# Sums of squares with the data as the stationary operand, and the engines that take the roots: a four-layer graph network on one core

## The chip, the cores and the metric

The kernel runs on one core of a Trainium2 chip. A core has five engines, each with its own in-order queue: TensorE (PE; its weight loads are shown as PEld), VectorE (DVE), ScalarE (ACT), GpSimd (POOL) and SyncE (SP), which here issues the transfers. The metric is the device time of one execution in microseconds, as a median over several runs.

## The reference, cut to what matters

64 graphs of 256 nodes with 128 features pass through four layers. Each layer's result is added to its input and normalised. What bears on this case:

```python
def _layernorm(x, axis=-1, eps=1e-5):
    return (x - mean(x)) / sqrt(var(x) + eps)

# layer 0: p = x (W1 - W2), q = x W2
h = max over j of relu(p_i + q_j + b) * adj[i, j]
# layer 1: three elu(x W + b), two products with adj, tanh of a product
# layer 2: a graph convolution with a normalised adjacency, used twice
A_hat = adj + eye;  deg = A_hat.sum(-1);  dinv = where(deg > 0, rsqrt(deg), 0)
norm_A = dinv[:, None] * A_hat * dinv[None, :]
# layer 3: one message per pair of nodes
pre = m_j[None, :, :] + m_i[:, None, :] + b1
msg = gelu(_layernorm(pre, g1, be1))          # variance over the 128 features
agg[i] = sum over j of msg[i, j] * adj[i, j]
x = _layernorm(x + _layernorm([x, agg] @ W2 + b2, g2, be2))
```

The adjacency holds zeros and ones, is symmetric, has a one on its diagonal, and about one entry in eight is set.

## The kernel before, in words

**Columns instead of pairs.** Layers 0 and 3 work on pairs of nodes. For each graph, and each half `h` (0 or 1) of its 256 source nodes, the target nodes are sorted by how many neighbours they have in that half (`perm`, `permT`). Then up to 40 slots are filled: slot `s` holds the `s`-th neighbour of each target, and as targets are sorted, high slots need few columns. All slots of one half stand side by side in 4800 columns (`WIDTH`), cut into tiles of 1024, 1024, 1024, 1024 and 704. `hot` is a matrix of zeros and ones, 128 sources by 4800 columns in fp8, made by DVE at L629 and L635; a product with `hot` gathers a neighbour's features into each column. A column whose target has fewer neighbours than its slot is empty: its column of `hot` is all zeros. `lack` (L591) says by how much a slot exceeds a target's count.

**Four stages.** `first` (L502) loads a graph, sorts, makes `hot` and does layer 0: three matmuls per 512 columns (L665), small ones that push empty columns far down (L681), and a running maximum on DVE (`fold`, L492). `second` is layer 1. `third` (L782) is layer 2 and the beginning of layer 3. `last` (L821) is the rest of layer 3 and the update. At any time the four stages work on four consecutive graphs. `together` (L341) takes the next piece of that stage which is least advanced by its share; the shares are the numbers of pieces in `STAGES` (L879), and a piece ends at a `yield`. This fixes, when the program is built, the order of the instructions on each engine. All graphs are unrolled.

**Layer 3 by tiles.** `TODO` lists ten tiles per graph (five per half). For each, `sums_of` (L718) gathers `c3` by three matmuls per 512 columns into a PSUM tile `bigp`, of which there are four (L728); DVE adds the target's part into `pre` (L732); ACT squares it into `sq` (L736). The features stand on the 128 partitions, so the sum over features is a product with ones: four matmuls per tile (L743), ones as the stationary operand (32 columns), a quarter of the squares as the moving one, each into its own 32 partitions of PSUM. ACT copies the sums into `row`, with 1/128 as scale and eps added (L745), and SP writes one row of each quarter to a line in DRAM (L750). After each second tile the line of both is read back across partitions, 16 values on each, as `vr` (L762); the mask `fu` comes beside it (L764); ACT takes the root and DVE the reciprocal (`inverse_root`, L72 to L75), DVE multiplies by the mask (L769), and the scales go to DRAM as `scale_line` (L771). `last` reads them back, broadcast to all partitions, as `rs_s` (`fetch`, L825), multiplies `pre` (L839), applies Gelu on ACT (L841) and sums over slots (`fold` again). `sums_of` runs four tiles ahead of this (`AHEAD`), and `fetch` two.

**The mask.** `first` compares `lack` with zero (L615) and writes the answer to DRAM in the order of the columns, in eight transfers (L620).

**Roots elsewhere.** `layernorm` (L166) adds eps on DVE (L174), yields, takes the root on ACT and the reciprocal on DVE, yields, and scales. It is called five times per graph. `layer_2` (L261) makes `dinv` from the degrees by the same `inverse_root`, adds the identity to `aT`, and scales `hs` by `dinv` on DVE before each of two products with `aT` (L293, L296). ACT keeps one set of functions loaded; where the next function is of another set, an ACT_TABLE_LOAD stands before it.

A second path, `general`, is there for inputs that the sparse one can't hold. It isn't run with these.

Of the kernel before, what the change touches and what calls it, by code (L numbers as in the profile page):

```python
# [19 lines left out]
P = 128  # L20
# [23 lines left out]
def kernel(  # L44
# [19 lines left out]
    make_identity(nc, ident)  # L64
    half = consts.tile([P, N], F32, name="half")
    nc.vector.memset(half, 0.5)
    eps_t = consts.tile([P, 1], F32, name="eps_t")
    nc.vector.memset(eps_t, EPS)
    minus1 = consts.tile([P, 1], F32, name="minus1")
    nc.vector.memset(minus1, -1.0)  # L70

    def inverse_root(t):  # L72

        nc.scalar.activation(t, t, AF.Sqrt)  # L74
        nc.vector.reciprocal(t, t)  # L75

# [80 lines left out]
    class Shared:  # L157
# [8 lines left out]
        def layernorm(self, dst, src, g=None, be=None):  # L166

            st = self.work.tile([P, H, 6], F32, name="st", bufs=4)
            mv = self.work.tile([P, H, 2], F32, name="mv", bufs=4)
            for h in range(H):  # L170
                nc.vector.bn_stats(st[:, h], src[:, h])
                nc.vector.bn_aggr(mv[:, h], st[:, h])
            rs = self.work.tile([P, H], F32, name="rs", bufs=4)
            nc.vector.tensor_scalar(rs, mv[:, :, 1], EPS, None, ALU.add)  # L174
            yield
            inverse_root(rs)
            yield
# [25 lines left out]
        def to_features(self, xn, name, bufs=None):  # L203

            pt = self.psum()
            for h in range(H):
                nc.tensor.transpose(pt[:, h * P:(h + 1) * P], xn[:, h], ident)
            t = self.state.tile([P, N], F32, name=name, **({"bufs": bufs} if bufs else {}))
            nc.scalar.copy(t, pt[:, :N])
            return t  # L210

        def node_tile(self, name):
# [47 lines left out]

        def layer_2(self, s, aT, deg_of):  # L261

            work, psum, elu = self.work, self.psum, self.elu
            x2 = s["x2"]
            deg = work.tile([P, H], F32, name="deg")
            deg_of(deg)
            nc.vector.tensor_scalar(deg, deg, 1.0, None, ALU.add)
            pos = work.tile([P, H], F32, name="pos")
            nc.vector.tensor_scalar(pos, deg, 0.0, None, ALU.is_gt)
            dinv = work.tile([P, H], F32, name="dinv")  # L270
            nc.vector.tensor_scalar(dinv, deg, 1e-30, None, ALU.max)
            inverse_root(dinv)
            yield
            nc.vector.tensor_mul(dinv, dinv, pos)
            for h in range(H):
                blk = aT[:, h, h * P:(h + 1) * P]
                nc.vector.tensor_add(blk, blk, ident)
            yield
            xT = self.to_features(x2, "xT_2", 1)
# [11 lines left out]
            for step in (1, 2):  # L291
                for h in range(H):
                    nc.vector.tensor_scalar(hs[:, h], hs[:, h], dinv[:, h:h + 1], None, ALU.mult)  # L293
                pa = psum()
# [59 lines left out]
    def sparse(ctx):  # L354
# [28 lines left out]
        def row_of(slot):  # L383
            return slot + 3 if slot < SLOTS - 1 else 0
# [109 lines left out]
        def split3(dst, src):  # L494
# [5 lines left out]
            nc.vector.tensor_sub(dst[:, 2], r, dst[:, 1])  # L500

        def first(g, s):  # L502

# [38 lines left out]
            nc.vector.scalar_tensor_tensor(kc, pc, -1.0, down_c, ALU.mult, ALU.subtract)  # L542
            dg = state.tile([P, H], F32, name="dg", bufs=3)
            nc.vector.tensor_reduce(dg, pc, AX.X, ALU.add)
            s["dg"] = dg

# [65 lines left out]
            s.update(an=an, aT=aT, perm=perm, permT=permT, lack=lack)  # L612

            full = pair.tile([ROWS, H, N], BF16, name="full")
            nc.vector.tensor_scalar(full, lack, 0.0, None, ALU.is_equal)  # L615
            s["fulls"] = fulls = dram.tile([H, WIDTH], BF16, name="fulls", bufs=5)
            for s0, n, w in RECTS:
                for a, m in ([(s0, n)] if s0 != g_s0 else [(s0, n - 1), (SLOTS - 1, 1)]):
                    at, r = SLOT_AT[a][0], row_of(a)
                    nc.sync.dma_start(  # L620
                        fulls[:, at:at + m * w].rearrange("h (s k) -> s h k", k=w), full[r:r + m, :, :w]
                    )
            yield
# [18 lines left out]
            yield  # L642
            s["hot"] = hot

            pq = psum()
# [66 lines left out]

        TODO = [(h, t0, tl) for h in range(H) for t0, tl in TILES]
        AHEAD = 4
        GROUP = 2
        PIECE = 16

        def sums_of(s, i):  # L718
# [5 lines left out]
            for b in range(0, tl, 512):  # L724
# [10 lines left out]
            sq = big.tile([P, TILE], F32, name="sq", bufs=1)  # L735
            nc.scalar.activation(sq[:, :tl], pre[:, :tl], AF.Square)  # L736
            yield

            bl = P if tl % 512 == 0 else tl // 4
            v4 = sq[:, :tl].rearrange("p (b q k) -> p b q k", q=4, k=bl)  # L740
            pr = psum()
            for q in range(4):
                nc.tensor.matmul(pr[q * Q:(q + 1) * Q, :tl // 4], ones[:, :Q], v4[:, :, q], start=True, stop=True)  # L743
            row = big.tile([P, TILE // 4], F32, name="row")
            nc.scalar.activation(row[:, :tl // 4], pr[:, :tl // 4], AF.Identity, bias=eps_t, scale=1.0 / P)  # L745
            at = sum(n for _, _, n in TODO[i - i % GROUP:i])
            if at == 0:
                s["line"] = dram.tile([1, GROUP * TILE], F32, name="line")
            line = s["line"]
            nc.sync.dma_start(  # L750
                line[:, at:at + tl].rearrange("o (b q k) -> (o q) b k", q=4, k=bl),
                row.rearrange("(q p) n -> q p n", p=Q)[:, 0, :tl // 4].rearrange("q (b k) -> q b k", k=bl),
            )
            yield
            if i % GROUP < GROUP - 1:
                return

            n = at + tl
            rows = n // PIECE
            first_at = TODO[i - GROUP + 1][0] * WIDTH + TODO[i - GROUP + 1][1]  # L760
            vr = big.tile([P, PIECE], F32, name="vr")
            nc.sync.dma_start(vr[:rows], line[:, :n].rearrange("o (p k) -> (o p) k", k=PIECE))  # L762
            fu = big.tile([P, PIECE], BF16, name="fu")
            nc.sync.dma_start(  # L764
                fu[:rows],
                s["fulls"].rearrange("h w -> (h w)")[first_at:first_at + n].rearrange("(p k) -> p k", k=PIECE),
            )
            inverse_root(vr[:rows])
            nc.vector.tensor_mul(vr[:rows], vr[:rows], fu[:rows])  # L769
            out_line = dram.tile([1, GROUP * TILE], F32, name="scale_line")  # L770
            nc.sync.dma_start(out_line[:, :n].rearrange("o (p k) -> (o p) k", k=PIECE), vr[:rows])  # L771
            at = 0
            for j in range(i - GROUP + 1, i + 1):
                s["scale", j] = out_line[:, at:at + TODO[j][2]]
                at += TODO[j][2]
            yield
# [5 lines left out]
        def third(g, s):  # L782

            dg = s["dg"]

            def deg_of(deg):
                nc.vector.tensor_scalar(deg, dg, 1.0 / N, None, ALU.mult)

            yield from sh.layer_2(s, s["aT"], deg_of)
            yield  # L790
# [30 lines left out]
        def last(g, s):  # L821
# [3 lines left out]
            def fetch(i):  # L825
                if i < len(TODO):
                    scale_of[i] = rs = big.tile([P, TILE], F32, name="rs_s", bufs=3)
                    nc.sync.dma_start(rs[:, :TODO[i][2]], s.pop(("scale", i)).broadcast_to([P, TODO[i][2]]))

# [48 lines left out]
        U = next(u for u in (UNROLL, 8, 4, 2, 1) if B % u == 0)  # L878
        STAGES = [(last, 34), (third, 34), (second, 14), (first, 44)]  # L879

# [14 lines left out]
    def general(ctx):  # L895
# [11 lines left out]
        psum = sh.psum  # L907
        ones3 = cs.tile([3, P], BF16, name="ones3")

        def split3(dst, src):  # L910
# [67 lines left out]
        def middle(g, s):  # L978
# [9 lines left out]

            def deg_of(deg):
                nc.vector.tensor_reduce(deg, an, AX.X, ALU.add)  # L990

            yield from sh.layer_1(s, an, aT, s["x1"])
            yield
            yield from sh.layer_2(s, aT, deg_of)
            yield

# [81 lines left out]
        def run():  # L1078
            nc.vector.memset(ones3, 1.0)

            with tc.For_i(0, B, U) as g0:
# [61 lines left out]
```

## Time and profile before

| what | value |
|---|---|
| median of three runs | 5727.86 us (5726.6 to 5728.21) |
| the profiled execution's own time | 5731.62 us |
| span from its first to its last instruction | 5729.7 us |
| mean granted clock of TensorE | 0.862 |
| DMA: mean busy share of the engines, rate | 20.0%, 63 GB/s |
| ACT_TABLE_LOAD at L841, L74, L194 | 535, 445, 221 of 1283 ns each |
| largest waits: ACT at L745 for L743 on PE | 476.7 us |
| PE at L296 for DVE at L293, at L769 | 214.8 us, 101.3 us |
| DVE at L839 for the transfer into rs_s | 48.0 us |

A line of groups gives the line of the code, the engine, the operation, output and input with their shapes, the count, then after the bar the busy time in us and the mean ns of one, then the idle time before them and what ended it. A line of the timeline gives the start in us, the length in us, the engine, the line, and how many instructions it merges. A line of stretches gives the stretch, its length, and the busy time of each engine in it, with counts in brackets, then the granted clock, the DMA share and the rate. Busy time of PE is the time in which at least one matmul is under way, from its start to its modelled end.

### The profile page before, as it was taken

To read this page: it belongs to the slowest core of one execution; us is meant where nothing else is said; L and a number is where in the kernel's file an instruction comes from. 1 tells how busy PE (TensorE), PEld (TensorE's weight loads), DVE (VectorE), ACT (ScalarE), POOL (GpSimd) and SP (SyncE) were. 2 spreads that over 40 slices of the span, in tenths; PEclk is the share of its full clock that TensorE was granted. 3 is DMA by queue.
4 is the path that set the end of the run, shared out by engine and by line. 5 is a ranking of instruction groups with operands and counts; after the bars stand their busy time and mean duration, and the time that the engine had idled before them with its cause. 6 is when DMAs were issued, how large, how long until landed. Compare 5 with 4: busy or idle time off the path is not lost.

```text
span 5729.7 us, 83531 instructions
## 1 busy us (share of the span) xinstructions
PE 4529.9 (79%) x27408; PEld 2508.7 (44%) x27408; DVE 4834.4 (84%) x14654; ACT 4275.2 (75%) x6485; POOL 1.9 (0%) x10
## 2 busy tenths in 40 slices
PE   5878878878778778788788788787887887877875
PEld 2444444444444444444444444444444444444443
DVE  6788888888888888888888888888888888888876
ACT  2577777777777777777777777777777777777785
POOL 0000000000000000000000000000000000000000
PEclk8888889889889889888898898898888887888986
DMA  0122222222212221221221222122212212221222
GB/s 22 44 70 63 62 63 72 62 63 66 69 57 70 65 63 63 72 63 62 63 72 62 63 65 70 59 68 65 63 62 72 64 62 63 69 66 60 68 65 74
DMA packets 292813, 365.15 MB, mean 64 GB/s; under 512 B 151952, under 2 KB 210448, under 8 KB 292368
## 3 DMA queue, kind: packets, MB, share of 16 engines
q1 hardware_dynamic: 292368, 359.73, 20.0%
q8 instruction: 217, 3.56, 0.3%
q14 instruction: 228, 1.87, 0.1%
HBM read 345.07 MB, written 14.53 MB: 63 GB/s over the span
## 4 chain that ended last, share of the span: by engine, by line
PE 52%; DVE 29%; ACT 11%; issue 4%; DMA 3%; SPq 0%; DVEq 0%; POOL 0%; ACTq 0%
PE bigp L665 11%; PE bigp L728 8%; DVE pre L839 6%; PE mm L860 5%; DVE lanes L492 4%; PE mm L743 4%; DVE hot L629 4%; DVE pre L732 4%; DVE sums L492 3%; PE bigp L681 3%; DMA rs_s<-scale_line 2%; PE mm L870 2%; PE mm L296 2%; PE mm L699 2%; PE mm L647 2%
## 5 line engine op out<-in xcount | busy, mean ns | idle before, releaser
L665 PE MATMUL bigp<-hot,q 128*128 128x512 fp8e4 (+1 forms) x3840 | 1052.3, 371 | 66.6 <-DVE lanes L492 52.6
L728 PE MATMUL bigp<-hot,c 128*128 128x512 fp8e4 (+1 forms) x3840 | 928.8, 372 | 140.2 <-DVE pre L732 140.2
L732 DVE TENSOR_TENSOR pre<-bigp,dT 128x512 f32<-128x512 f32 (+6 forms) x1664 | 846.3, 530 | 37.8 <-PE bigp L728 33.5
L492 DVE TENSOR_TENSOR lanes<-bigp,lanes 128x512 f32<-128x512 f32 (+6 forms) x1536 | 772.7, 503 | 94.6 <-PE bigp L681 86.9
L839 DVE TENSOR_TENSOR pre<-pre,rs_s 128x1024 f32<-128x1024 f32 (+1 forms) x640 | 732.9, 1150 | 48.6 <-DMA rs_s<-scale_line 48.0
L736 ACT ACTIVATE sq<-pre 128x1024 f32<-128x1024 f32 (+1 forms) x640 | 638.5, 998 | 169.9 <-DVE pre L732 163.9
L841 ACT ACT_TABLE_LOAD x535 | 686.4, 1283 | 9.5
L492 DVE TENSOR_TENSOR sums<-pre,sums 128x1024 f32<-128x1024 f32 (+6 forms) x1024 | 628.8, 614 | 41.2 <-ACT pre L841 40.7
L745 ACT ACTIVATE row<-mm,eps_t 128x256 f32<-128x256 f32 (+1 forms) x640 | 289.6, 453 | 476.9 <-PE mm L743 476.7
L841 ACT ACTIVATE pre<-pre,be,g 128x1024 f32<-128x1024 f32 (+1 forms) x512 | 594.2, 1172 | 57.8 <-DVE pre L839 53.0
L743 PE MATMUL mm<-sq,ones 128*32 128x256 f32 (+1 forms) x5120 | 482.9, 440 | 135.2 <-ACT sq L736 135.2
L74 ACT ACT_TABLE_LOAD x445 | 570.9, 1283 | 7.5
L728 PEld LDWEIGHTS <-c 128*128 128x128 bf16 x3840 | 331.2, 98 | 550.5 <-issue 136.1
L665 PEld LDWEIGHTS <-q 128*128 128x128 bf16 x3840 | 310.8, 97 | 392.6 <-issue 112.0
L296 PE MATMUL mm<-aT,hs 128*128 128x256 f32 x512 | 232.3, 600 | 316.1 <-DVE hs L293 214.8
L629 DVE TENSOR_SCALAR hot<-rank 128x512 fp8e4<-128x512 bf16 (+5 forms) x1536 | 440.5, 348 | 0.0
L681 PEld LDWEIGHTS <-pick 42*128 42x128 bf16 x2944 | 155.8, 95 | 481.5 <-issue 474.2
L296 PEld LDWEIGHTS mm<-aT,hs 128*128 128x128 f32 x512 | 135.6, 293 | 425.8 <-issue 316.1
L860 PE MATMUL mm<-w3u,sums 128*128 128x128 f32 x2048 | 296.7, 289 | 18.4 <-DVE sums L492 16.1
L194 ACT ACT_TABLE_LOAD x221 | 283.5, 1283 | 3.9
L681 PE MATMUL bigp<-lack,pick 42*128 42x36 bf16 (+16 forms) x2944 | 285.7, 187 | 0.0
L860 PEld LDWEIGHTS mm<-w3u,sums 128*128 128x128 f32 x2048 | 254.5, 195 | 37.3 <-issue 17.6
(226 smaller groups left out, 7132.6 us busy)
## 6 DMA issues: line engine op xcount, KB each, us to landing
rs_s<-scale_line SPq DMA_DIRECT2D x512, 512.0 KB
rs_s<-scale_line SPq DMA_DIRECT2D x128, 352.0 KB
an<-in_adj SPq DMA_DIRECT2D x64, 256.0 KB
x<-in_x SPq DMA_DIRECT2D x64, 128.0 KB
line<-row SPq DMA_DIRECT2D x512, 4.0 KB
out<-o SPq DMA_DIRECT2D x64, 128.0 KB
fu<-fulls SPq DMA_DIRECT2D x192, 4.0 KB
vr<-line SPq DMA_DIRECT2D x192, 8.0 KB
```

The lines of the kernel that those rows point to most:

```text
L74: nc.scalar.activation(t, t, AF.Sqrt)
L492: nc.vector.tensor_tensor(lanes[:, :k, :w], src[:, i:i + k], lanes[:, :k, :w], op)
L629: nc.vector.tensor_scalar(hot[:, :, at:at + w], rank[:, :, :w], s0 + i + 1.0 - FAR, None, ALU.is_equal, saturate=False)
L665: nc.tensor.matmul(pt[:, :tl], q3[:, i, h], hot[:, h, t0:t0 + tl], start=i == 0, stop=False)
L681: nc.tensor.matmul(o_, l_, r_, start=False, stop=i == len(todo) - 1)
L728: nc.tensor.matmul(pt[:, :bl], c3[:, k, h], hot[:, h, t0 + b:t0 + b + bl], start=k == 0, stop=k == 2)
L732: nc.vector.tensor_add(block(pre[:, b:], n, w, at), block(pt, n, w, at), widen(dT[:, h, :w], n))
L736: nc.scalar.activation(sq[:, :tl], pre[:, :tl], AF.Square)
L743: nc.tensor.matmul(pr[q * Q:(q + 1) * Q, :tl // 4], ones[:, :Q], v4[:, :, q], start=True, stop=True)
L839: nc.vector.tensor_mul(pre[:, :tl], pre[:, :tl], rs[:, :tl])
L841: nc.scalar.activation(msg[:, :tl], pre[:, :tl], AF.Gelu, bias=be3, scale=g3)
L860: nc.tensor.matmul(pt[:, cols], lanes[:, k, cols], w3u[:, 1], start=k == 0, stop=False)
```

## The change

1. The squares become the stationary operand. `sums_of` picks every eighth column of `sq` from column `b` on, for `b` from 0 to 7 (`PIECE`), as a stationary block of 128 columns, and multiplies by one column of ones. The sums come out with 128 columns of the tile on the partitions and eight per partition, in the arrangement that `vr` had after its way through DRAM. ACT copies them into `vr` (scale and eps as before). The lines `line`, `row` and `fu` and their transfers go.
2. The mask comes from `hot` itself: its column sums by TensorE, 80 matmuls per graph of the same kind with two columns of ones, copied by DVE into `filled`. The comparison and the eight transfers go, and `first` has one piece more (45).
3. The scales' root is one POOL instruction (power -0.5), and the product with the mask is POOL's too. Each tile has its own scale line.
4. `dinv` is made in `first`, with the power on POOL, and scales `aT` once instead of `hs` twice.
5. The norms' root stays on ACT, with eps as its bias; the add on DVE goes, and the reciprocal moves past a yield.
6. `sq` has two buffers instead of one.

```diff
     def inverse_root(t):
-        nc.scalar.activation(t, t, AF.Sqrt)
-        nc.vector.reciprocal(t, t)
+        nc.gpsimd.tensor_tensor(t, t, mhalf[:t.shape[0], :t.free_size()], ALU.pow)
...
+            yield
             rs = self.work.tile([P, H], F32, name="rs", bufs=4)
-            nc.vector.tensor_scalar(rs, mv[:, :, 1], EPS, None, ALU.add)
-            yield
-            inverse_root(rs)
-            yield
+            nc.scalar.activation(rs, mv[:, :, 1], AF.Sqrt, bias=eps_t)
+            yield
+            nc.vector.reciprocal(rs, rs)
...
+        def inverse_root_of(self, deg, bufs):
+            nc.vector.tensor_scalar(deg, deg, 1.0, None, ALU.add)
+            pos = self.work.tile([P, H], F32, name="pos")
+            nc.vector.tensor_scalar(pos, deg, 0.0, None, ALU.is_gt)
+            dinv = self.state.tile([P, H], F32, name="dinv", bufs=bufs)
+            nc.vector.tensor_scalar(dinv, deg, 1e-30, None, ALU.max)
+            inverse_root(dinv)
+            nc.gpsimd.tensor_mul(dinv, dinv, pos)
+            return dinv
...
+            for h in range(H):
+                nc.vector.tensor_scalar(aT[:, h], aT[:, h], dinv[:, h:h + 1], None, ALU.mult)
...
             for step in (1, 2):
-                for h in range(H):
-                    nc.vector.tensor_scalar(hs[:, h], hs[:, h], dinv[:, h:h + 1], None, ALU.mult)
...
-            full = pair.tile([ROWS, H, N], BF16, name="full")
-            nc.vector.tensor_scalar(full, lack, 0.0, None, ALU.is_equal)
-            s["fulls"] = fulls = dram.tile([H, WIDTH], BF16, name="fulls", bufs=5)
...
+            pf = psum()
+            for i, (h, t0, tl) in enumerate(TODO):
+                for b in range(PIECE):
+                    c = (i * PIECE + b) * 2
+                    nc.tensor.matmul(
+                        pf[:tl // PIECE, c:c + 2], hot[:, h, t0 + b:t0 + tl:PIECE], ones_b[:, :2], start=True, stop=True
+                    )
+            filled = hold.tile([P, H, len(TILES), PIECE], F32, name="filled")
...
+        def scale_root(t, full):
+            nc.gpsimd.tensor_tensor(t, t, mhalf3[:t.shape[0], :t.shape[1]], ALU.pow)
+            nc.gpsimd.tensor_mul(t, t, full)
...
             pr = psum()
-            for q in range(4):
-                nc.tensor.matmul(pr[q * Q:(q + 1) * Q, :tl // 4], ones[:, :Q], v4[:, :, q], start=True, stop=True)
-            row = big.tile([P, TILE // 4], F32, name="row")
-            nc.scalar.activation(row[:, :tl // 4], pr[:, :tl // 4], AF.Identity, bias=eps_t, scale=1.0 / P)
...
+            rows = tl // PIECE
+            for b in range(PIECE):
+                nc.tensor.matmul(pr[:rows, b:b + 1], sq[:, b:tl:PIECE], ones[:, :1], start=True, stop=True)
+            if i % GROUP == 0:
+                s["vr"] = big.tile([P, GROUP, PIECE], F32, name="vr")
+            vr = s["vr"]
+            nc.scalar.activation(vr[:rows, i % GROUP], pr[:rows, :PIECE], AF.Identity, bias=eps_t[:rows], scale=1.0 / P)
...
+            for j in range(i0, i + 1):
+                s["scale", j] = line = dram.tile([1, TILE], F32, name="scale_line")
+                nc.sync.dma_start(
+                    line[:, :TODO[j][2]].rearrange("o (p k) -> (o p) k", k=PIECE), vr[:all_rows[j - i0], j - i0]
+                )
...
-        STAGES = [(last, 34), (third, 34), (second, 14), (first, 44)]
+        STAGES = [(last, 34), (third, 34), (second, 14), (first, 45)]
```

More of the change, by code (lines that the diff above doesn't have):

```diff
@@ L64 @@
     make_identity(nc, ident)
-    half = consts.tile([P, N], F32, name="half")
-    nc.vector.memset(half, 0.5)
     eps_t = consts.tile([P, 1], F32, name="eps_t")
@@ L70 @@
     nc.vector.memset(minus1, -1.0)
+    mhalf = consts.tile([P, 16], F32, name="mhalf")
+    nc.vector.memset(mhalf, -0.5)
+    mhalf3 = mhalf.rearrange("p (a b) -> p a b", a=2)
     def inverse_root(t):
-        nc.scalar.activation(t, t, AF.Sqrt)
-        nc.vector.reciprocal(t, t)
+        nc.gpsimd.tensor_tensor(t, t, mhalf[:t.shape[0], :t.free_size()], ALU.pow)
     def load(src, shape, name):
@@ L259, in layer_1, with layer_2 @@
             s["x2"] = x2
-        def layer_2(self, s, aT, deg_of):
+        def layer_2(self, s, aT, dinv_of):
             work, psum, elu = self.work, self.psum, self.elu
             x2 = s["x2"]
[L265 to L272, printed above, removed]
+            dinv = dinv_of()
             yield
-            nc.vector.tensor_mul(dinv, dinv, pos)
             for h in range(H):
@@ L500, in split3 @@
             nc.vector.tensor_sub(dst[:, 2], r, dst[:, 1])
+        TODO = [(h, t0, tl) for h in range(H) for t0, tl in TILES]
+        AHEAD = 4
+        GROUP = 2
+        PIECE = 8
         def first(g, s):
@@ L542, in first @@
             nc.vector.scalar_tensor_tensor(kc, pc, -1.0, down_c, ALU.mult, ALU.subtract)
-            dg = state.tile([P, H], F32, name="dg", bufs=3)
+            dg = work.tile([P, H], F32, name="dg")
             nc.vector.tensor_reduce(dg, pc, AX.X, ALU.add)
-            s["dg"] = dg
+            nc.vector.tensor_scalar(dg, dg, 1.0 / N, None, ALU.mult)
+            s["dinv"] = sh.inverse_root_of(dg, 4)
             more = work.tile([P, H, H], F32, name="more")
@@ L612, in first @@
             s.update(an=an, aT=aT, perm=perm, permT=permT, lack=lack)
-            full = pair.tile([ROWS, H, N], BF16, name="full")
-            nc.vector.tensor_scalar(full, lack, 0.0, None, ALU.is_equal)
-            s["fulls"] = fulls = dram.tile([H, WIDTH], BF16, name="fulls", bufs=5)
[L617 to L622, printed above, removed]
             yield
@@ L643, in first @@
             s["hot"] = hot
+            pf = psum()
[6 more added lines that the diff above has]
+            filled = hold.tile([P, H, len(TILES), PIECE], F32, name="filled")
+            pfv = pf[:, :2 * len(TODO) * PIECE].rearrange("p (h t b two) -> p h t b two", h=H, b=PIECE, two=2)[..., 0]
+            rows = TILES[-1][1] // PIECE
+            last_t = len(TILES) - 1
+            nc.vector.tensor_copy(filled[:, :, :last_t], pfv[:, :, :last_t])
+            nc.vector.tensor_copy(filled[:rows, :, last_t], pfv[:rows, :, last_t])
+            s["filled"] = filled.rearrange("p h t b -> p (h t) b")
+            yield
             pq = psum()
@@ L711, in first @@
             yield from sh.layernorm(s["x1"], y)
[L713 to L716, printed above, removed]
+        def scale_root(t, full):
+            nc.gpsimd.tensor_tensor(t, t, mhalf3[:t.shape[0], :t.shape[1]], ALU.pow)
+            nc.gpsimd.tensor_mul(t, t, full)
         def sums_of(s, i):
@@ L734, in sums_of @@
                     )
-            sq = big.tile([P, TILE], F32, name="sq", bufs=1)
+            sq = big.tile([P, TILE], F32, name="sq")
             nc.scalar.activation(sq[:, :tl], pre[:, :tl], AF.Square)
             yield
-            bl = P if tl % 512 == 0 else tl // 4
-            v4 = sq[:, :tl].rearrange("p (b q k) -> p b q k", q=4, k=bl)
             pr = psum()
-            for q in range(4):
-                nc.tensor.matmul(pr[q * Q:(q + 1) * Q, :tl // 4], ones[:, :Q], v4[:, :, q], start=True, stop=True)
-            row = big.tile([P, TILE // 4], F32, name="row")
-            nc.scalar.activation(row[:, :tl // 4], pr[:, :tl // 4], AF.Identity, bias=eps_t, scale=1.0 / P)
[L746 to L753, printed above, removed]
+            rows = tl // PIECE
[5 more added lines that the diff above has]
+            nc.scalar.activation(vr[:rows, i % GROUP], pr[:rows, :PIECE], AF.Identity, bias=eps_t[:rows], scale=1.0 / P)
             yield
@@ L756, in sums_of @@
                 return
[L758 to L775, printed above, removed]
+            i0 = i - GROUP + 1
+            all_rows = [TODO[j][2] // PIECE for j in range(i0, i + 1)]
+            parts = [(all_rows[0], 0, GROUP)] if len(set(all_rows)) == 1 else [
+                (r, j, j + 1) for j, r in enumerate(all_rows)
+            ]
+            for r, lo, hi in parts:
+                scale_root(vr[:r, lo:hi], s["filled"][:r, i0 + lo:i0 + hi])
+            for j in range(i0, i + 1):
[3 more added lines that the diff above has]
+                )
             yield
@@ L782, in third @@
         def third(g, s):
[L784 to L789, printed above, removed]
+            yield from sh.layer_2(s, s["aT"], lambda: s["dinv"])
             yield
@@ L827, in fetch @@
                     scale_of[i] = rs = big.tile([P, TILE], F32, name="rs_s", bufs=3)
-                    nc.sync.dma_start(rs[:, :TODO[i][2]], s.pop(("scale", i)).broadcast_to([P, TODO[i][2]]))
+                    nc.sync.dma_start(rs[:, :TODO[i][2]], s.pop(("scale", i))[:, :TODO[i][2]].broadcast_to([P, TODO[i][2]]))
             for i in range(2):
@@ L908, in general @@
         ones3 = cs.tile([3, P], BF16, name="ones3")
+        half = cs.tile([P, N], F32, name="half")
         def split3(dst, src):
@@ L987, in middle, with dinv_of @@
             yield
-            def deg_of(deg):
+            def dinv_of():
+                deg = work.tile([P, H], F32, name="deg")
                 nc.vector.tensor_reduce(deg, an, AX.X, ALU.add)
+                return sh.inverse_root_of(deg, 1)
             yield from sh.layer_1(s, an, aT, s["x1"])
             yield
-            yield from sh.layer_2(s, aT, deg_of)
+            yield from sh.layer_2(s, aT, dinv_of)
             yield
@@ L1079, in run @@
             nc.vector.memset(ones3, 1.0)
+            nc.vector.memset(half, 0.5)
             with tc.For_i(0, B, U) as g0:
```

## The prediction

> **What bounds the kernel now.** I read the page's first two parts, then the busy time by stretch of one graph's interval, then single rows for prices. The program repeats per graph: the four matmuls of L566 start first at 43.2 us and last at 5456.2 us (view of that line), (5456.2 - 43.2) / 63 = 85.9 us per graph. I cut one interval, 2853.44 to 2939.44 us, where PE's character changes.
>
> ```profile
> PE 4529.9 (79%) x27408; PEld 2508.7 (44%) x27408; DVE 4834.4 (84%) x14654; ACT 4275.2 (75%) x6485; POOL 1.9 (0%) x10
> ```
> ```profile
> 2853.44:2857.44 4.00, 4.00 (x11) 3.28 (x11) 1.71 (x4) 0.63 (x3) 0.00 (x0) 0.50 0.50 166
> 2857.44:2905.44 48.00, 47.32 (x315) 26.60 (x318) 43.00 (x131) 34.13 (x49) 0.00 (x0) 1.00 0.23 69
> 2905.44:2939.44 34.00, 18.02 (x110) 9.06 (x109) 29.72 (x95) 31.66 (x51) 0.00 (x0) 0.80 0.13 42
> ```
> The columns are the length, then busy time of PE, PEld, DVE, ACT, POOL, then the granted clock. The average (PE 79%) hides two stages. In the 48 us, **stage A**, PE is covered for 47.3 and DVE for 43.0: these two set the pace and ACT (34.1) follows. In the 34 us, **stage B**, ACT (31.7) and DVE (29.7) set it and PE is half idle. PE's cover in A is flattered, because pipelined matmuls overlap. Counting its matmuls there by column count at their dense spacing (512 columns of fp8: 0.216 us, the median from start to start of L665; fp32 128 columns: 0.111) gives 38.5 us, of which the sums of squares (L743) are 2.2. So A has 9.5 us in which PE streams nothing.
>
> **The sums of squares on PE.** Before, one tile of 1024 columns costs eight matmuls that run four abreast:
>
> ```profile
> L743 PE MATMUL mm<-sq,ones 128*32 128x256 f32 (+1 forms) x5120 | 482.9, 440 | 135.2 <-ACT sq L736 135.2
> 2811.18 0.64 PE L743 MATMUL mm<-sq,ones 128*32 128x256 f32 x8
> ```
> That is 482.9 / 64 = 7.5 us per graph. After, the data are stationary: eight blocks per tile, each an fp32 block of 128 columns picked with a step of 8 elements, streaming one column. Every fp32 matmul here is two instructions (L743: 5120 for 640 x 4), so 16 load-and-multiply pairs per tile, 11 equivalents in the two 704-column tiles (88 of 128 stationary columns): 8 x 16 + 2 x 11 = 150 per graph. With one column to stream, a pair costs its weight load. The rows that price it:
>
> ```profile
> 2808.97 0.97 PEld L870 LDWEIGHTS mm<-ak,permT 128*128 128x128 f32 x8
> L870 PEld LDWEIGHTS mm<-ak,permT x1024: 186/192/333, 278.9 to 5718.2; 128*128 128x128 f32 x171
> 2835.44 1.16 PE L566 MATMUL mm<-perm,nz 128*128 128x256 bf16 x4 [4.15 <-DVE perm L560]
> L488 DVE TENSOR_REDUCE part_max<-bigp x128: 344/357/358, 64.8 to 5518.6; 128x12 f32<-128x192 f32 x128
> L488 DVE TENSOR_REDUCE part_add<-pre x128: 448/476/491, 253.9 to 5707.4; 128x12 f32<-128x192 f32 x128
> ```
> Contiguous fp32 loads follow each other every (0.97 - 0.192) / 7 = 0.111 us: the lower end. No row has a weight load with a 32-byte step. Two rows show what steps do to reads. L566 streams 256 bf16 columns 4 bytes apart: (1.16 - 0.372) / 3 = 0.263 us each, 1.03 ns per element; 128 elements make 0.131. L488 reduces 192 elements with a step of 48 bytes: 476 ns from SBUF; the same shape from PSUM takes 357. A two-element reduce takes 152 (L544), so SBUF costs (476 - 152) / 192 = 1.69 ns per element; 128 make 0.216: the upper end. I take **0.216**, because its step passes 16 bytes as the new one does (32), and L566's 4 do not. Per graph: 150 x 0.111 = 16.7, x 0.131 = 19.7, x 0.216 = 32.4 us, in place of 7.5.
>
> The Trainium skill (SBUF — State Buffer, Door 1: The DMA port swizzle) speaks against the change: SBUF has 16-byte lines, fp32 strides of up to four elements are free, and each access to a new line pays. It names no size. By it the load is above 0.111 us; L488 agrees in direction, and no run here shows it for TensorE.
>
> **Stage A, the term that decides.** Six of a graph's ten tiles lie there (48 weight loads of L743), 96 pairs. PE's dense sum without the old ones is 38.5 - 2.2 = 36.3. With them: 47.0 at 0.111, 48.9 at 0.131, 57.0 at 0.216. At 0.216 PE alone passes the stage's 48 us. A burst is 16 x 0.216 = 3.5 us, while the four bigp buffers hold DVE for about 4 x 0.55 = 2.2 us (L732, L492 at 0.53 and 0.50), so DVE stands still in each. I add 2 us for waits that stay: 59, **+11 us**.
>
> **The mask of full columns** adds 80 pairs per graph: fp8 blocks, two moving columns. Nearest: L599's four bf16 loads in 0.18 us, one lasting 0.104, so 0.025 us apart; with L488's 1.69 ns on a quarter of the columns (32) 0.054. So 2 to 4.3 us, I take 3. They wait for the last hot (L635) and stand ahead of L647 in PE's queue; PE sat idle there anyway, waiting for DVE before L296: (214.8 + 101.3) / 64 = 4.9 us per graph. Without that cover they cost their 3 us. Two DVE copies from PSUM add 2 x 0.16 (L604) to 2 x 0.28 (L656).
>
> **ACT.** These rows show one removed root:
>
> ```profile
> 2859.93 1.28 ACT L74 ACT_TABLE_LOAD   x1
> 2861.22 0.21 ACT L74 ACTIVATE vr<-vr 128x16 f32<-128x16 f32 x1
> 2862.89 1.28 ACT L841 ACT_TABLE_LOAD   x1
> ```
> The root brings a table load before it and one for the next Gelu. In this interval's order on ACT, striking the five scale roots and the degree root takes away 8 loads: six in A (ACT isn't the bound: free), two in B. That is 10.3 us of ACT; six root activations are 1.3 more. The copy from PSUM (L745, 453 ns at 256 columns) becomes 8 columns wide, about 0.2: 10 x 0.25 = 2.5. ACT in B falls by 2.6 + 0.4 + 1.0 = 4.0 to 27.7.
>
> The Trainium skill (ScalarE: Activation LUTs, What ACT_TABLE_LOAD costs) adds a drain of about 1380 ns to the 1283 of a load. The rows differ: the root starts 1.29 us after its load. By the page the eight would be worth 21 us.
>
> **DVE** loses L174 (0.80), reciprocals and mask products of scales (1.23 + 0.83), degrees (0.25), L615 (0.28), and L293 (0.95); it gains two scalings of aT (0.6, by L197 at 0.29) and the copies (0.3 to 0.6): net -3.3 us, some 2 in A, 1.3 in B. Degree steps move from the third stage to the first at the same cost. In the norms one DVE step goes and their chain keeps its root on ACT.
>
> **GpSimd and SP.** Power on POOL is in no row. Its nearest is L392, 128x128 in 0.39 us: 0.05 for 16 columns below, ten times the row, 4 us, above; I take 0.5. Behind it in POOL's queue stand only the next product and roots; for it waits the scale line's DMA. SP's issues fall from 33 to 10 per graph (10 line, 5 vr, 5 fu, 8 fulls, 5 scale lines, against 10 scale lines), and a round trip through DRAM goes. DVE's waits for rs_s are only 48.0 / 64 = 0.75 us per graph, and a scale is fetched two tiles ahead (2 x 86 / 10 = 17 us), so 4 us hide.
>
> **Stage B**: PE 14.3 (dense count) - 2.5 + 4 x 3.5 + 3 = 28.8 of 34; ACT 27.7; DVE 28.4. It is a chain of waits, so I count -1 (from -3 to +2). The first 4 us, matmuls at clock 0.50, might run warmer: -0.5 (0 to -2).
>
> **Sum**: 11 - 1 - 0.5 = +9.5 us per graph, x 64 = +608. The profiled execution took 5731.6 (span 5729.7), 3.8 over the median shown, 5727.86. Forecast **6340**, own range 6120 to 6600 (6 to 13.5 us per graph).
>
> **Rivals.**
> 1. *Faster:* the step costs weight loads nothing. At 0.111 stage A's PE sum is 47.0, inside 48; a burst is 1.8 us, under the buffers' 2.2, and DVE's relief decides: -2.2 us per graph, 5590. For it: PE's 9.5 us gap. Against: L488. It turns at a pair of (48 - 36.3) / 96 = 0.122 us.
> 2. *Little slower:* pairs at 0.111 to 0.131, but a third of the old gaps stays: A 50 to 52, B -1.5: about +1.6, 5830 (5700 to 6050).
> 3. *The clock:* bursts of single columns count as idle. In 2925.44:2929.44 the granted clock was 0.50, after 4 us with PE busy for 1.29. If A's other 36 us run cold for a fifth of their work, 7 us are added: 6790.
> 4. *GpSimd is slow:* a root beyond 17 us makes L839 wait; at 4 us per graph on the forecast, 6600. That the roots don't leave ACT is excluded: the diff issues them on POOL.
>
> **How the numbers follow.** Forecast 0.42, rival 1 0.25, rival 2 0.18 (0.04 of it within 0.2%), rival 3 0.12, rival 4 0.03. A measurement here can tell about 0.2%, 11 us. Faster 0.25, same 0.04, slower 0.71. The range from 5560 to 6750 leaves out rival 1's far end (0.06) and the upper half of rivals 3 and 4 with the forecast's tail (0.12).
>
> **What would show it.** Right: the new matmuls' group has weight loads of about 0.2 us spacing, some 32 us per graph, PE covered nearly throughout, DVE waiting on bigp in A. Loads at 0.11 spacing mean rival 1 or 2; a granted clock of 0.5 inside the stage means rival 3; L839 waiting for rs_s means rival 4. L74's loads should fall, the total by about eight per graph. If PE turns out to hide a burst's loads behind earlier streams, the prediction is wrong.

## The result and the profile after

The changed kernel takes 8580.1 us (median of four runs, 8573.4 to 8592.6) against 5728.0: a ratio of 1.498, 95% interval 1.495 to 1.501. Slower was forecast, but 6340 with a range to 6750; the time lies far outside it. The page of the changed kernel, first the engines' busy time, then the granted clock in tenths over 40 slices, then five groups:

```profile
PE 7419.7 (87%) x37648; PEld 5412.5 (63%) x37648; DVE 4850.1 (57%) x13502; ACT 3709.9 (43%) x5749; POOL 1201.5 (14%) x1034
PEclk8676676676766767667667677676766767667676
L756 PEld LDWEIGHTS mm<-ones,sq 128*128 128x128 f32 x10240 | 2355.4, 320 | 66.5 <-ACT sq L751 20.9
L730 POOL TENSOR_TENSOR vr<-vr,mhalf 128x16 f32<-128x16 f32 (+2 forms) x448 | 1025.4, 2289 | 7125.6 <-ACT vr L760 7125.6
L835 DVE TENSOR_TENSOR pre<-pre,rs_s 128x1024 f32<-128x1024 f32 (+1 forms) x640 | 737.1, 1152 | 447.5 <-DMA rs_s<-scale_line 445.9
L760 ACT ACTIVATE vr<-mm,eps_t 128x8 f32<-128x8 f32 (+1 forms) x640 | 170.8, 267 | 2364.8 <-PE mm L756 1480.7
L496 DVE TENSOR_TENSOR lanes<-bigp,lanes 128x512 f32<-128x512 f32 (+6 forms) x1536 | 783.6, 510 | 1050.0 <-PE bigp L697 1022.7
```
PE's busy time grew by 2890 us, a little more than the time itself (2852); DVE's is unchanged and ACT's fell by 565. The weight loads of the new sums take 2355 / 64 = 36.8 us per graph. But PE's other work grew too: the clock's digits are mostly 6 and 7, where the kernel before had a mean of 0.862; the mean now is 0.707. DVE waits 445.9 us for the scales, where it waited 48.0, and 1022.7 us for PE at L496, where it waited 86.9. And ACT waits 1480.7 us for the new sums, where it waited 476.7 for the old ones.

One graph's interval of the changed kernel, from the start of the second L300 group of a graph to the end of L308, to the end of the L715 matmuls (stage A), to the start of the next graph's second L300 group (stage B). The cuts before were at the same places to 0.6 us. First all engines, then the new sums alone (PE, PEld):

```profile
3978.83:3987.05 8.22, 8.22 (x94) 7.30 (x94) 3.83 (x10) 6.32 (x8) 0.00 (x0) 0.50 0.43 130
3987.05:4058.54 71.49, 70.68 (x344) 49.16 (x342) 38.40 (x109) 20.04 (x33) 6.79 (x6) 0.77 0.10 32
4058.54:4111.35 52.81, 36.73 (x157) 28.02 (x156) 33.15 (x92) 31.84 (x50) 11.81 (x10) 0.65 0.13 43
```
```profile
3978.83:3987.05 8.22, 0.21 (x2) 0.41 (x2) 0.50 0.43 130
3987.05:4058.54 71.49, 17.73 (x82) 18.16 (x81) 0.77 0.10 32
4058.54:4111.35 52.81, 17.93 (x80) 18.22 (x80) 0.65 0.13 43
```
Stage A went from 48.0 to 71.5 us and is covered by PE throughout. Stage B went from 34.0 to 52.8 with PE covered for only 36.7 of it. Its growth, 18.8, is close to what the new pairs take there (17.9), though PE had seemed half idle; that the two agree is chance, since e9 below has the same pairs and a stage B of 45.8. The first stretch doubled by the mask, whose 80 matmuls stand in it:

```profile
3980.70 3.58 PE L649 MATMUL mm<-ones_b,hot 128*128 128x2 bf16 x80
```

The same cuts through every trace, as medians over 55 graphs, in us (half speed is the share of the stretch with a granted clock of 0.5):

| kernel | time | first stretch | stage A | stage B | half speed in A, in B |
|---|---|---|---|---|---|
| before | 5728 | 4.3 | 48.4 | 34.6 | 0.00, 0.52 |
| changed | 8580 | 8.2 | 71.6 | 53.2 | 0.45, 0.71 |
| e1: neighbouring columns | 7323 | 8.2 | 54.9 | 49.6 | 0.15, 0.70 |
| e3: wide | 7272 | 8.2 | 56.7 | 47.1 | 0.03, 0.36 |
| e9: roots on ACT | 7981 | 8.2 | 68.8 | 45.8 | 0.36, 0.77 |
| e11: e9 and wide | 7179 | 7.5 | 56.9 | 46.1 | 0.03, 0.37 |
| e2: bf16 | 6436 | 8.2 | 47.5 | 42.9 | 0.03, 0.80 |
| e6: bf16, old mask | 6355 | 4.5 | 48.4 | 44.6 | 0.00, 0.75 |
| e5: bf16, roots on ACT | 5803 | 8.2 | 46.9 | 33.6 | 0.06, 0.59 |
| e7: norms and degrees | 5726 | 4.6 | 49.5 | 33.2 | 0.02, 0.50 |
| e8: e7 with bf16 | 5794 | 4.5 | 48.2 | 35.8 | 0.01, 0.70 |

### The profile page after: what moved, and what is told of

Read it like the earlier page. It is cut to its first block, busy times and chain, and to the rows that moved or that the text cites. A ratio compares the mean times of both kernels' runs of the same rounds, so it can differ in the third digit from the quotient of the medians.

```text
span 8572.4 us, 101172 instructions
## 1 busy us (share of the span) xinstructions
PE 7419.7 (87%) x37648; PEld 5412.5 (63%) x37648; DVE 4850.1 (57%) x13502; ACT 3709.9 (43%) x5749; POOL 1201.5 (14%) x1034
## 5 line engine op out<-in xcount | busy, mean ns | idle before, releaser
L756 PEld LDWEIGHTS mm<-ones,sq 128*128 128x128 f32 x10240 | 2355.4, 320 | 66.5 <-ACT sq L751 20.9
L756 PE MATMUL mm<-ones,sq 128*128 128x1 f32 x10240 | 2296.1, 354 | 5.4 <-ACT sq L751 5.4
L730 POOL TENSOR_TENSOR vr<-vr,mhalf 128x16 f32<-128x16 f32 (+2 forms) x448 | 1025.4, 2289 | 7125.6 <-ACT vr L760 7125.6
L496 DVE TENSOR_TENSOR lanes<-bigp,lanes 128x512 f32<-128x512 f32 (+6 forms) x1536 | 783.6, 510 | 1050.0 <-PE bigp L697 1022.7
L743 PE MATMUL bigp<-hot,c 128*128 128x512 fp8e4 (+1 forms) x3840 | 1161.7, 455 | 148.2 <-DVE pre L747 142.6
L681 PE MATMUL bigp<-hot,q 128*128 128x512 fp8e4 (+1 forms) x3840 | 1193.3, 427 | 46.4 <-DVE lanes L496 43.3
L760 ACT ACTIVATE vr<-mm,eps_t 128x8 f32<-128x8 f32 (+1 forms) x640 | 170.8, 267 | 2364.8 <-PE mm L756 1480.7
L835 DVE TENSOR_TENSOR pre<-pre,rs_s 128x1024 f32<-128x1024 f32 (+1 forms) x640 | 737.1, 1152 | 447.5 <-DMA rs_s<-scale_line 445.9
L743 PEld LDWEIGHTS <-c 128*128 128x128 bf16 x3840 | 430.6, 121 | 682.3 <-issue 310.9
L496 DVE TENSOR_TENSOR sums<-pre,sums 128x1024 f32<-128x1024 f32 (+6 forms) x1024 | 633.0, 618 | 29.7 <-ACT pre L837 23.9
L300 PE MATMUL mm<-aT,hs 128*128 128x256 f32 x512 | 264.2, 671 | 344.3 <-DVE hs L202 344.2
L856 PE MATMUL mm<-w3u,sums 128*128 128x128 f32 x2048 | 406.4, 361 | 9.6 <-DVE sums L496 9.6
L208 PE MATMUL mm<-ident,x 128*128 128x128 f32 x512 | 172.8, 412 | 255.4 <-DVE x L181 255.4
L300 PEld LDWEIGHTS mm<-aT,hs 128*128 128x128 f32 x512 | 151.9, 327 | 373.8 <-DVE hs L202 338.8
L856 PEld LDWEIGHTS mm<-w3u,sums 128*128 128x128 f32 x2048 | 354.0, 260 | 29.2 <-issue 22.4
```

What stands on the lines that cost most here:

```text
L300: nc.tensor.matmul(pa[:, :N], hs[:, h], aT[:, h], start=h == 0, stop=h == H - 1)
L496: nc.vector.tensor_tensor(lanes[:, :k, :w], src[:, i:i + k], lanes[:, :k, :w], op)
L681: nc.tensor.matmul(pt[:, :tl], q3[:, i, h], hot[:, h, t0:t0 + tl], start=i == 0, stop=False)
L730: nc.gpsimd.tensor_tensor(t, t, mhalf3[:t.shape[0], :t.shape[1]], ALU.pow)
L743: nc.tensor.matmul(pt[:, :bl], c3[:, k, h], hot[:, h, t0 + b:t0 + b + bl], start=k == 0, stop=k == 2)
L756: nc.tensor.matmul(pr[:rows, b:b + 1], sq[:, b:tl:PIECE], ones[:, :1], start=True, stop=True)
```

## The experiments

Theory A: the price of the new weight loads, and the clock that they leave behind. Its first rival, theory B: the scales' way through GpSimd. Later, theory C: the mask's matmuls and the new order.

**e1, contiguous blocks.**
```diff
-nc.tensor.matmul(pr[:rows, b:b + 1], sq[:, b:tl:PIECE], ones[:, :1], start=True, stop=True)
+nc.tensor.matmul(pr[:rows, b:b + 1], sq[:, b * rows:(b + 1) * rows], ones[:, :1], start=True, stop=True)
```


> The changed kernel with one edit: each stationary block of squares is 128 neighbouring columns in place of every eighth one (the scales then reach the wrong columns; the work is the same in kind and amount). Theory A, the weight loads and the clock that they leave: with the 32-byte step gone a load falls from the 0.237 us of the changed kernel to the 0.111 (full clock) to 0.213 (half clock) of the contiguous fp32 loads before, so the 150 pairs of a graph fall from 36 us to 17 to 32, and the time from 8580 us to 7300 to 8100, the more the more the clock recovers. Theory B, the chain of the scales through GpSimd (power of 2.3 us, DVE waiting 446 us for rs_s): 8400 to 8600, since that chain is untouched. If the step does nothing, the spacing of the loads stays at 0.237 us.

Measured: 7322.6 us, clock 0.771, a single execution. From start to start a load takes 0.112 us at full clock and 0.213 at half (medians); in the changed kernel 0.237 at either. So the step of 32 bytes doubles the load at full clock, and A's expectation holds. The order of the instructions on PE, ACT and DVE is that of the changed kernel, so the 1258 us are the step's, with the clock that shorter loads leave.

**e2, squares in bf16.**
```diff
-sq = big.tile([P, TILE], F32, name="sq")
+sq = big.tile([P, TILE], BF16, name="sq")
-nc.tensor.matmul(pr[:rows, b:b + 1], sq[:, b:tl:PIECE], ones[:, :1], start=True, stop=True)
+nc.tensor.matmul(pr[:rows, b:b + 1], sq[:, b:tl:PIECE], ones_b[:, :1], start=True, stop=True)
```


> The changed kernel with the squares in bf16 and ones in bf16: one pass instead of two, and a load of the kind that the mask's have in the changed kernel (0.033 us apart). All else is as in the changed kernel. Theory A: 75 pairs of about 0.033 to 0.054 us, some 3 to 4 us per graph in place of 36, the clock back at 0.85 or more, and 5500 to 5850 us. Theory B: at least 8000 us, as the power, the queue of SP and the order of the work are unchanged.

Measured: 6436.1 us, ratio 1.124 (1.121 to 1.127). The loads come 0.060 us apart and the matmuls cost 489.5 us in all, what the old ones cost (482.9). Stage A is back at 47.5. Yet 700 us stay: theory A alone is refuted, and most of them stand in stage B, at 42.9.

**e3, a wide moving operand.**
```diff
-nc.tensor.matmul(pr[:rows, b:b + 1], sq[:, b:tl:PIECE], ones[:, :1], start=True, stop=True)
+nc.tensor.matmul(pr[:rows, b:b + P], sq[:, b:tl:PIECE], ones, start=True, stop=True)
```


> The changed kernel with 128 columns of ones as the moving operand in place of one; each product overwrites all but the first of the columns of the one before, so the sums are the same. The weight loads are untouched. The clock part of theory A: the streams run beside the next load (0.107 us at full and 0.213 at half clock, both under 0.237), the array is seen as busy, the granted clock rises from 0.707 to over 0.9, and the other streams give back about 13 us per graph: 7500 to 8000 us, though the kernel does more. If the clock has no part in it, 8500 to 8700; if the streams do not hide beside the loads, 9000 and more.

Measured: 7271.8 us, clock 0.882, a single execution. The loads are as before; the two lines are this run's and the changed kernel's:

```profile
L756 PEld LDWEIGHTS mm<-ones,sq x10240: 238/334/343, 192.5 to 7236.8; 128*128 128x128 f32 x157, 128*88 128x88 f32 x40
```
```profile
L756 PEld LDWEIGHTS mm<-ones,sq x10240: 238/335/343, 187.6 to 8540.4; 128*128 128x128 f32 x157, 128*88 128x88 f32 x40
```
Smallest, median and largest duration agree, so nothing was saved on the loads, and PE streams 128 times the columns. Still the time falls by 1308 us, more than expected, and the share of half speed in stage A falls from 0.45 to 0.03. With one column per load the clock stood low there, though PE was covered throughout. The Trainium skill (TensorE: Matmul & The Clock Gate, Part 1) says that the clock follows how busy the array was in the last few microseconds. The run agrees if streaming is what counts and weight loads do not. The fall is not the clock's alone, though: the build with the wide operand also put ACT's and DVE's instructions in another order (ACT has 1007 table loads in place of 884). The clock's part is seen best in PE's busy time without the sums, for the same number of matmuls: 7420 - 2296 = 5124 us in the changed kernel, 6399 - 2418 = 3981 here.

**e4, the rest of the change alone.** From the kernel before: powers on GpSimd for scales and degrees, norms and `aT` as in the change; sums and mask as before. Of the edit, the scales' part (`inverse_root` and the product):
```diff
-        nc.scalar.activation(t, t, AF.Sqrt)
-        nc.vector.reciprocal(t, t)
+        nc.gpsimd.tensor_tensor(t, t, mhalf[:t.shape[0], :t.free_size()], ALU.pow)
...
-            nc.vector.tensor_mul(vr[:rows], vr[:rows], fu[:rows])
+            nc.gpsimd.tensor_mul(vr[:rows], vr[:rows], fu[:rows])
```


> The kernel before with the rest of the change and neither new use of TensorE: scales' and degrees' roots as powers on GpSimd with the product there, norms' root with eps as bias, aT scaled once; the sums by ones as stationary operand, the line through DRAM and the mask by transfers as before. Theory A: the rest costs nothing or gains, 5450 to 5750 us, with about 8 table loads less per graph. Theory B: a good part of the loss is here, 6300 us or more.

Measured: 5829.4 us, ratio 1.018 (1.015 to 1.020): between the two expectations, a loss of 101 us. DVE's wait for rs_s is 303.5 us.

**e5, bf16 squares with the scales' roots on ACT and DVE.**
```diff
-            nc.gpsimd.tensor_tensor(t, t, mhalf3[:t.shape[0], :t.shape[1]], ALU.pow)
-            nc.gpsimd.tensor_mul(t, t, full)
+            nc.scalar.activation(t, t, AF.Sqrt)
+            nc.vector.reciprocal(t, t)
+            nc.vector.tensor_mul(t, t, full)
```


> The run with bf16 squares (6436 us) with the scales' roots back on ACT (Sqrt) and DVE (reciprocal, product with the mask); degrees' roots stay on GpSimd. Theory B, GpSimd's chain of the scales: in that run a power takes 1.6 to 2.9 us, 4.7 beside DVE's making of hot, DVE waits 587 us for rs_s (9.2 per graph) and PE behind it; with a root of 0.2 and a reciprocal of 0.25 us these waits fall under 150 us and the time to 5700 to 5950 us, though some 7 table loads per graph come back. Theory C, the mask's 80 matmuls and the new order hold the 600 us over the run of the rest alone: 6350 to 6500 us.

Measured: 5802.8 us, ratio 1.013 (1.011 to 1.015): 633 us under e2, and nearly all of it in stage B (42.9 to 33.6). DVE's wait for rs_s falls from 586.6 to 8.1 us. Theory B holds for this part. How it comes about shows in e2's timeline, GpSimd and then DVE (lines between left out):

```profile
3006.94 4.80 POOL L730 TENSOR_TENSOR vr<-vr,mhalf 128x8 f32<-128x8 f32 x1 [6.91 <-ACT vr L760]
3011.82 2.19 POOL L731 TENSOR_TENSOR vr<-vr,filled 128x8 f32<-128x8 f32 x1
3013.97 2.90 POOL L730 TENSOR_TENSOR vr<-vr,mhalf 128x16 f32<-128x16 f32 x1
```
```profile
3007.59 3.43 DVE L629 TENSOR_SCALAR hot<-rank 128x512 fp8e4<-128x512 bf16 x10
3012.22 1.72 DVE L629 TENSOR_SCALAR hot<-rank 128x512 fp8e4<-128x512 bf16 x8
3019.04 1.22 DVE L835 TENSOR_TENSOR pre<-pre,rs_s 128x1024 f32<-128x1024 f32 x1 [3.21 <-DMA rs_s<-scale_line]
3023.39 1.23 DVE L835 TENSOR_TENSOR pre<-pre,rs_s 128x1024 f32<-128x1024 f32 x1 [1.46 <-DMA rs_s<-scale_line]
```
In this run a power of eight columns takes 1.64 us, and 4.70 (medians of 67 and 61) where DVE is making hot for more than half of it; the product after it 0.20 and 2.19. The scales of a tile and of the next pair leave GpSimd one after the other, land by 3019, and DVE stands at L835, with the rest of its queue behind it. The Trainium skill (GPSIMD Engine Reference, 8. Key points) says that GpSimd shares its SBUF interfaces with VectorE and collides with some of its instructions. These numbers agree.

**e6, bf16 squares with the mask by transfers,** the comparison and eight transfers of the kernel before, read per tile (lines joined, the rest left out):
```diff
-            nc.tensor.matmul(pf[:tl // PIECE, c:c + 2], hot[:, h, t0 + b:t0 + tl:PIECE], ones_b[:, :2], start=True, stop=True)
...
+            nc.sync.dma_start(fu[:all_rows[j - i0], j - i0], flat[c0:c0 + TODO[j][2]].rearrange("(p k) -> p k", k=PIECE))
```


> The run with bf16 squares (6436 us) with the mask by comparison and transfers as in the kernel before, in place of the 80 matmuls per graph and their two copies; roots stay on GpSimd. Theory C: the matmuls stand for 3.4 us per graph on the path between the last hot and L663, beside a colder clock: 6436 - 64 x 3.6 = 6200 us or less. Theory B: within 100 us of 6436, or slower by the transfers that stand in SP's queue.

Measured: 6354.8 us, ratio 1.110 (1.108 to 1.111): 81 us under e2, where theory C wanted 230 or more. The first stretch gives back its 3.7 us, stage B takes 1.7 of them and stage A 0.9. Theory C is a small part.

**e7, norms and degrees alone:** e4 with the scales' roots as before.
```diff
-            inverse_root(vr[:rows])
-            nc.gpsimd.tensor_mul(vr[:rows], vr[:rows], fu[:rows])
+            nc.scalar.activation(vr[:rows], vr[:rows], AF.Sqrt)
+            nc.vector.reciprocal(vr[:rows], vr[:rows])
+            nc.vector.tensor_mul(vr[:rows], vr[:rows], fu[:rows])
```


> The kernel before with only the norms' root with eps as bias and the degrees made early (power on GpSimd, aT scaled once); sums, mask and scales' roots as before. Theory B: what the run of the rest alone loses (5829 against 5728) is the scales' power on GpSimd; without it DVE has 2.3 us per graph less (L174 0.8, L293 0.95 - 0.6, L615 stays) and ACT two table loads less: 5560 to 5700 us. If the order or the early degrees cost something: 5750 and more.

Measured: 5726.3 us, ratio 0.999 (0.998 to 1.000): no difference. So e4's loss is the power on GpSimd, as theory B said, but the gain expected from DVE's lighter load is not there.

**e8, e7 with squares in bf16,** ones still stationary.
```diff
-            sq = big.tile([P, TILE], F32, name="sq", bufs=1)
+            sq = big.tile([P, TILE], BF16, name="sq")
...
-                nc.tensor.matmul(pr[q * Q:(q + 1) * Q, :tl // 4], ones[:, :Q], v4[:, :, q], start=True, stop=True)
+                nc.tensor.matmul(pr[q * Q:(q + 1) * Q, :tl // 4], ones_b[:, :Q], v4[:, :, q], start=True, stop=True)
```


> The run before this one with the squares and ones in bf16, ones still the stationary operand: each of four matmuls per tile becomes one instruction of 256 columns instead of two at half rate. PE's 7.5 us per graph for the sums fall to some 2.5, six tenths of it in stage A. If PE holds stage A: 2 to 3 us per graph, 130 to 190 us under the run before this one; if DVE holds it: within 60 us.

Measured: 5794.2 us, ratio 1.011 (1.010 to 1.013): slower than e7 with less work on PE. Both expectations miss. Stage A falls by 1.3 us, but stage B grows by 2.6, and DVE's wait for rs_s goes from 14.8 to 100.3 us. `sq` also has two buffers here, ACT's and DVE's instructions stand in another order (1021 table loads against 1085), and the clock is lower (0.824 against 0.865). No run separates these.

**e9, the changed kernel with the scales' roots on ACT and DVE** (the edit of e5, squares in fp32).

> The changed kernel (fp32 squares as stationary blocks, step of 8) with the scales' roots on ACT and DVE; nothing else differs. With bf16 squares this edit was worth 633 us. If the two costs add (loads and clock; GpSimd's chain): 8580 - 633 = 7950 us. If PE's loads cover GpSimd's lateness: 8450 to 8600. If the lateness makes PE idle and so cold as well: under 7900.

Measured: 7981.4 us, a single execution: 599 under the changed kernel, near the 633 with bf16 squares. With a narrow operand the two costs add. Against e5, with the same 847 table loads and nearly the same order, fp32 squares lengthen stage A by 21.9 us and stage B by 12.2.

**e11, e9 with the wide moving operand** (the edit of e3).

> The run before this one with 128 columns of ones as the moving operand: the loads stay at 0.237 us, the clock is kept up. With GpSimd and the clock both taken out, what is left over the kernel before is PE's own time for the 150 pairs and the mask, 35.5 + 3.6 - 7.5 = 31.6 us per graph, where nothing hides it: at most 5728 + 64 x 31.6 = 7750; since stage A had 9.5 us in which PE streamed nothing, and B 16 of 34 uncovered, 6700 to 7100 us is expected. If the clock isn't a cost of its own, no less than the run before.

Measured: 7179.4 us, clock 0.892, a single execution: a little over the expected span. Against e9 stage A gives back 12.0 us and stage B nothing. The order on ACT and DVE changed here as well, and more: ACT has 1390 table loads in place of 847.

**e10, e5 with the wide moving operand in bf16.**
```diff
-nc.tensor.matmul(pr[:rows, b:b + 1], sq[:, b:tl:PIECE], ones_b[:, :1], start=True, stop=True)
+nc.tensor.matmul(pr[:rows, b:b + P], sq[:, b:tl:PIECE], ones_b, start=True, stop=True)
```


> The run with bf16 squares and roots on ACT (5803 us, clock 0.825) with 128 columns of ones as moving operand (0.053 us at full clock, under the 0.060 of a load). If the colder clock (half speed for 35% of the time against 28% in the kernel before) is what that run still loses: 5650 to 5750 us and a clock of 0.86 or more. If not: 5790 to 5850.

Measured: 5801.1 us, ratio 1.012 (1.011 to 1.014), clock 0.878 against 0.825. The second expectation holds: the clock rose and the time stayed. With bf16 loads, where stage A is no longer than before the change, the colder clock costs nothing that shows.

**e12, e10 with the mask's matmuls widened too.**
```diff
-pf[:tl // PIECE, c:c + 2], hot[:, h, t0 + b:t0 + tl:PIECE], ones_b[:, :2], start=True, stop=True
+pf[:tl // PIECE, c:c + P], hot[:, h, t0 + b:t0 + tl:PIECE], ones_b, start=True, stop=True
```


> The run before this one with the mask's 80 matmuls widened to 128 columns as well (0.053 us each at full, 0.107 at half clock, against 0.033 now). They stand where PE waits for DVE and the clock is low: if warming it there pays the matmuls behind them (L663, L300 at half speed), 50 to 130 us under the run before this one; if they only last longer, 80 x 0.02 to 0.07 = 1.6 to 5.9 us per graph, 100 to 350 us over it.

Measured: 5799.7 us, ratio 1.012 (1.010 to 1.014): the same as e10; neither expectation holds.

**The sum.** From the changed kernel by e9 and e11 to e10, each step one edit: GpSimd's roots 599, the wide operand 802, bf16 squares 1378, together 2779. The steps add up because they follow one another; the check is in the rest, since e10 stands 73 us over the kernel before, and the mask, which it keeps, costs 81 by e6. The shares depend on the path. With the wide operand first, that step is 1308 (changed to e3) and GpSimd's roots are only 92 (e3 to e11), so what GpSimd's lateness costs is not one number. And the wide runs changed the order of instructions too, which the pieces of `together` alone do not fix: the 802, the 92 and the 1378 hold that as well. PE's busy time without the sums still tells the clock's part: 7300 - 2343 = 4957 us in e9, 6411 - 2436 = 3975 in e11. Free of the order, or nearly, are fp32 against bf16 squares at one column, loads and clock together: 2144 us (changed to e2) and 2179 (e9 to e5).

No version beats the kernel before: e7 equals it, and e5 without its mask would come to 5803 - 81 = 5722 by subtraction, which wasn't run.

## Why the prediction was wrong, point by point

By the medians the forecast missed some 36 us per graph: 20 in stage B, 12 in stage A, 4 in the first stretch.

- **The price of a pair was about right,** but partly by luck: 0.216 us was taken from VectorE's strided reads in L488, another engine. 0.237 was measured, and 0.112 without the step (e1). 32.4 us per graph were forecast for the sums, 36.8 measured.
- **Stage A, "+11 us", was about right for what it counted.** Five tiles' sums lie there, not six (80 loads of 160), each dearer than forecast. With the clock kept A grows by 8.3 (e3) or 8.5 (e11), and DVE waits on bigp as forecast. But rival 3, the clock, was not a rival: it is a consequence of the same bursts and adds some 12 us in A (e11 to e9). It stood at 0.12 and 7 us, outside the sum.
- **Stage B, "so I count -1", is the step that failed.** It grew by 18.6 us (medians). The prediction called B a chain of waits, yet its sum set PE's total against the stage's length, 28.8 of 34, as if PE's idle time could be filled. PE's queue is in order, and its idle time was waiting inside that chain: a burst that starts in a gap is in the way of the matmul for which DVE or ACT waits next. ACT's queue is in order too: its copy of a burst's sums (L760) waits for the burst, and whatever stands behind the copy waits with it. In the changed kernel two bursts after 4090 stand on both sides of L300, PE first, then ACT (lines between left out):

```profile
4090.24 3.94 PE L756 MATMUL mm<-ones,sq 128*128 128x1 f32 x16
4094.05 2.06 PE L300 MATMUL mm<-aT,hs 128*128 128x256 f32 x4
4095.89 3.76 PE L756 MATMUL mm<-ones,sq 128*128 128x1 f32 x16
4100.32 1.22 PE L308 MATMUL mm<-w,agg 128*128 128x128 f32 x4 [0.67 <-ACT agg L303]
```
```profile
4088.06 0.42 DVE L202 SCALAR_TENSOR_TENSOR hs<-hs,elu_e 128x256 f32<-128x256 f32 x1
4094.22 0.27 ACT L760 ACTIVATE vr<-mm,eps_t 128x8 f32<-128x8 f32 x1 [3.19 <-PE mm L756]
4099.74 0.27 ACT L760 ACTIVATE vr<-mm,eps_t 128x8 f32<-128x8 f32 x1 [3.31 <-issue]
4099.90 0.36 ACT L303 COPY agg<-mm 128x256 f32<-128x256 f32 x1
```
  L300's input `hs` was ready at 4088.5, but L300 starts only when the first burst ends. L308, on which layer 2 goes on, comes 4.2 us after L300 had ended, though ACT's copy between them (L303) takes 0.36: that copy stands behind L760, which waits for the second burst (the profile names no releaser there; the burst ends at 4099.65). Five bursts lie in B, not four as forecast. Cheap loads take B's growth away only together with GpSimd's roots (e5, 33.6). From there fp32 loads, with the clock that they leave, add 12.2 (e9) and GpSimd's roots 7.4 more (changed). With the wide operand GpSimd's part of B is only 1.0 (e3 less e11), and what remains over the kernel before is 11.5 (e11).
- **GpSimd, "so 4 us hide", was wrong.** The price (1.6 to 2.9 us for a power, up to 4.9 in the changed kernel, against 0.5 taken and 4 as the upper end) lay near the upper end, and the cover was too short. Two tiles ahead is 17 us only if tiles come evenly. In the changed kernel's stage B they don't:

```profile
4064.76 1.20 DVE L835 TENSOR_TENSOR pre<-pre,rs_s 128x1024 f32<-128x1024 f32 x1
4067.13 1.22 DVE L835 TENSOR_TENSOR pre<-pre,rs_s 128x1024 f32<-128x1024 f32 x1
4072.46 1.23 DVE L835 TENSOR_TENSOR pre<-pre,rs_s 128x1024 f32<-128x1024 f32 x1 [2.92 <-DMA rs_s<-scale_line]
4075.37 1.22 DVE L835 TENSOR_TENSOR pre<-pre,rs_s 128x1024 f32<-128x1024 f32 x1
```
  Two tiles are about 8 us here, the wait included, and in e2 two scales also stand one behind the other on GpSimd. The point of 17 us for rival 4 rests on the same error: no root took 17 us, and L835 waited all the same.
- **The mask, 3 us under cover:** the matmuls take 231 us, 3.6 per graph, within the bounds of its price; the cover was not there (first stretch +3.9). It costs 81 us of time by e6.
- **ACT's table loads:** 8 fewer per graph were counted by striking roots from one interval's order. Measured 884 in place of 1236, 5.5 per graph; the order around them had changed. Little hung on it: e5 has 847 loads, 500 us of ACT's time less than before, and its stages A and B are within 1.5 us of the old ones.
- **The chances:** the parts that stood as rivals 3 and 4 (0.12, 0.03) both came true beside the forecast, rival 4 without its condition of 17 us. They shared no condition that excluded one another, so they were terms, and the range should have reached their sum: 6340 + 450 + 260 = 7050, and more with B.

## What to carry to other kernels

Before filling an engine's idle time with new work, ask who waits behind the slot: in an in-order queue a gap within a chain of waits isn't spare, and much of the new work's length may be added. Look at the other engines' queues as well: a copy that waits for the new work holds up what stands behind it. When one column is streamed per weight load, price the load at the step of its operand and ask what the clock will make of the whole stage. When runs are compared step by step, see whether the build kept the order of the instructions. Rivals that can be true together belong into the sum.

## What the runs showed of the hardware

- An fp32 weight load of 128 columns 32 bytes apart takes 0.237 us from start to start at full and at half clock (changed kernel); with neighbouring columns 0.112 and 0.213 (e1).
- The granted clock was 0.707 with 1 column streamed per load (changed kernel) and 0.882 with 128, the loads alike (e3).
- A power on GpSimd takes 0.70 us for 2 columns, 1.64 for 8 and 2.90 for 16, and 4.70 for 8 beside VectorE's bf16 to fp8 compares; a product of 8 columns 0.20 and 2.19 (e2).
- Halving TensorE's busy time on the sums (447.6 to 208.8 us, e7 to e8) came with a kernel 1.2% slower; buffers and order differ too. Why is open.
